# A convolution over edges: messages kept in PSUM, the radial layers moved two groups ahead, chunk sums turned in the messages' banks

## The chip, the core and the metric

The kernel runs on one core of one Trainium2 chip. The metric is the device time of one execution in microseconds (us). Before the change three runs took 5604.22, 5641.0 and 5611.24 us; the median is 5611.24.

The engines are called as in the profile: PE is TensorE (matmuls; PEld its weight loads), DVE is VectorE, ACT is ScalarE, POOL is GpSimd, SP is SyncE. In this kernel SP only issues DMAs and POOL issues the gathers (indirect DMAs).

## What is computed

Two graph layers over 6250 nodes of 128 features and 200000 edges, sorted by destination. The first is a pair of attention layers. The second, the one that is changed, is a convolution over the edges. Cut to what matters:

```python
h = maximum(layernorm(x), 0)
e0, e1 = f0[src], f1[src]            # the source node's features, 32 and 32 x 3, after a linear map
a0, a1 = attr4[:, 0], attr4[:, 1:4]  # four attributes of each edge
h = gelu(gelu(attr8 @ W_mlp1) @ W_mlp2)        # two layers on eight more attributes
w = einsum('pxu,ex->epu', W_tp, h)             # third layer: four weights of 32 each
m0 = w[:, 0] * e0 * a0
m1 = w[:, 3] * (e1 * a1).sum(-1)
m2 = w[:, 1] * e0 * a1                          # 3 x 32
m3 = w[:, 2] * e1 * a0                          # 3 x 32
agg = zeros.at[dst].add(concatenate([m0, m1, m2, m3]))    # 256 sums for each node
out = cos * s + sin * (agg @ Wf)                # s: a linear map of the node itself
x = x + out
```

Each edge so needs one gathered row of 128 numbers, three small matrix products, 256 products and one addition into its destination.

## The kernel before, in words

The attention layers fill the first 2430 us and are not touched, but for the pool from which their one-hot tiles come. The convolution reads `table3` (the mapped features of every node) from device memory.

The 200000 edges lie in 1563 tiles of 128, one edge in each partition. Eight tiles are a **group** (195 full groups, and one of three tiles). Thirty tiles are a **chunk**: the edges of a chunk go to nodes that lie within 128 of the chunk's first one, so one accumulator of 128 x 512 in PSUM (`whole`, one buffer) holds the sums of a chunk. There are 53 chunks.

For each group, in the program's order (`convolve`, from line 1236):

1. POOL issues eight gathers (`gather`, line 319), each of 128 rows of `table3` into `G` (six buffers).
2. PE and ACT run two layers: a matmul of 512 columns (line 1244), a gelu (1246), again a matmul (1248) and a gelu (1250). The matmuls write `small` tiles, two buffers of one bank. The third layer is sixteen or so matmul instructions of 128 columns (1256) into `pw`, shown as `big`: 128 x 1024 in two banks, two buffers.
3. ACT scales each tile of `G` by `a0` into `g0` (1267, eight operations).
4. DVE forms the products: `dot` = e1 * a1 (1269), its sum (1271), `w1` = w * e0 (1273), two products into `mid`, 128 x 1024 in SBUF (1274, 1275), and two in place into `big` (1278, 1279). `mid` and `big` together are the group's messages.
5. `halve` splits a number into a rounded part and a remainder, so that the scatter's matmuls may run in their faster format: ACT copies into the first half (335), DVE subtracts that from the number into the second (336). This is done for `mid`, then the one-hot tile of the next group is made (`one_hot`, 328, shown as `ohr`), then it is done for `big`.
6. PE scatters: for each tile one matmul of 512 columns (1286) with the one-hot tile as weights, added in `whole`. The two halves of messages lie beside each other and are added later.

At a chunk's end (`close`, `sums3`) ACT copies 256 columns of `whole` (1313) and DVE adds the other 256 (1314). The next chunk's first matmul into `whole` waits for that. In the seventh tile of the next chunk the sums are carried into its accumulator by a matmul with a shifted one-hot tile (`same`, 1344 and 1345). One group later `finish3` (1291) turns the sums by two transposes (1295, into a `small` tile), ACT copies them (1297), PE multiplies by `Wf` (1300) and DVE scales by sin and adds the node's own part `xb`, which SP loaded, in two operations (1303, 1304). SP stores the result.

SP issues, for each group, two loads of `attr8` (`a8t`, four buffers), for each five groups a load of `attr4` (`a4`, three buffers), for each chunk the load of `xb` and the store. DVE copies the three attributes `a1` of five groups from `a4` into PSUM (1362), in a bank `kept` that also holds the column numbers `slot` which `one_hot` compares with.

The order of instructions on each engine is set when the kernel is built: a scheduler takes the program's order as priority and puts an instruction earlier on its engine where it expects that engine free and the operands ready. Each engine runs its list strictly in that order, and waits are semaphores. A new tile in a pool waits until the last readers of the buffer that it takes over are done.

Of the kernel before, what the change touches and what calls it, by code (L numbers as in the profile page):

```python
# [42 lines left out]
P = 128  # L43
SB = 8
# [22 lines left out]
def gnn_kernel(ctx: ExitStack, tc: tile.TileContext, x, src, dst, attr4, attr8,  # L67
# [255 lines left out]
    def one_hot(dl, n, exact=True):  # L323
        if exact:
            oh = work.tile([P, SB, P], F32R, name="ohr", bufs=3)
        else:
            oh = gen.tile([P, GSB, P], F32, name="ohg")
        nc.vector.tensor_tensor(oh[:, :n, :], slot[:, None, :].to_broadcast([P, n, P]),
                                dl[:, :, None].to_broadcast([P, n, P]), op=OP.is_equal)
        return oh  # L330
# [26 lines left out]
    def attend(G, dl, n, oht, pq, H, acc_of, start, stop):  # L357
# [3 lines left out]
        oh = one_hot(dl, n)  # L361
# [24 lines left out]
    def attend_general(G, dl, n, erc, H, acc, start, stop):  # L386


        oh = one_hot(dl, n, False)
# [23 lines left out]
    def node_max(G, dl, n, H, most):  # L413

        oh = one_hot(dl, n, False)
# [633 lines left out]
    ps_big = ctx.enter_context(tc.tile_pool(name="ps_big", bufs=2, space=PSUM))  # L1049
    ps_sm = ctx.enter_context(tc.tile_pool(name="ps_sm2", bufs=2, space=PSUM))  # L1050
    ps_two = ExitStack()
    ps_bank = ps_two.enter_context(tc.tile_pool(name="ps_bank2", bufs=1, space=PSUM))
# [179 lines left out]
    kept = ctx.enter_context(tc.tile_pool(name="ps_kept", bufs=1, space=PSUM)).tile([P, 512], F32, name="kept")  # L1232
# [3 lines left out]
    def convolve(G, n, a0, a1, a8t, sink, oh, then=None):  # L1236


# [4 lines left out]
        ph = small()  # L1243
        nc.tensor.matmul(ph[:, :npr * P], wm1_sb[:rows], a8t[:rows, :npr * P], start=True, stop=True)  # L1244
        hid1 = cw.tile([2 * HID, NPR * P], F32, name="hid1")
        nc.scalar.activation(hid1[:, :npr * P], ph[:, :npr * P], AF.Gelu_apprx_tanh, scale=1.0 / math.sqrt(NRAD))  # L1246
        ph = small()
        nc.tensor.matmul(ph[:, :npr * P], wm2_sb, hid1[:, :npr * P], start=True, stop=True)  # L1248
        hid2 = cw.tile([2 * HID, NPR * P], F32, name="hid2")
        nc.scalar.activation(hid2[:, :npr * P], ph[:, :npr * P], AF.Gelu_apprx_tanh, scale=1.0 / math.sqrt(HID))  # L1250
        pw = big()

        for j in range(npr):
            for c in range(j, n, NPR):
                half = slice(c // NPR * HID, (c // NPR + 1) * HID)
                nc.tensor.matmul(pw[:, c, :], hid2[half, j * P:(j + 1) * P],  # L1256
                                 wtp_sb[half].rearrange("x p u -> x (p u)"), start=True, stop=True)
        w = pw[:, :n, :].rearrange("e c (p u) -> e c p u", p=4)
        m = cw.tile([P, SB, 4, MUL], F32, name="mid")
# [13 lines left out]
        nc.vector.tensor_tensor(w1[:, :n], w[:, :, 1, :], e0, op=OP.mult)  # L1273
        nc.vector.tensor_tensor(m[:, :n, 0, :], w[:, :, 3, :], dot1[:, :n], op=OP.mult)
        nc.vector.tensor_tensor(m[:, :n, 1:, :], w[:, :, 2, :][:, :, None, :].to_broadcast(s4),  # L1275
                                g0[:, :n, MUL:].rearrange("e c (i u) -> e c i u", i=3), op=OP.mult)

        nc.vector.tensor_tensor(w[:, :, 0, :], w[:, :, 0, :], g0[:, :n, :MUL], op=OP.mult)
        nc.vector.tensor_tensor(w[:, :, 1:, :], w1[:, :n, None, :].to_broadcast(s4),  # L1279
                                a1[:, :, :, None].to_broadcast(s4), op=OP.mult)  # L1280
        halve([ms[:, :n, j, 1] for j in range(2)], m[:, :n])
        got = then and then()
        halve([ms[:, :n, j, 0] for j in range(2)], w)
        for c in range(n):
            acc, start, stop = sink(c)
            nc.tensor.matmul(acc, oh[:, c, :], ms[:, c].rearrange("e s h i u -> e (s h i u)"), start=start, stop=stop)  # L1286
        return got

    sin = math.sin(math.pi / 8.0) / math.sqrt(2.0 * MUL) / math.sqrt(20.0)

    def finish3(a, xb, to):

        pt = small()
        for j in range(2):
            nc.tensor.transpose(pt[:, j * D:(j + 1) * D], a[:, j * D:(j + 1) * D], ident)
        at = cw.tile([P, 2, D], F32, name="at")
        nc.scalar.copy(at, pt[:, :2 * D].rearrange("p (j f) -> p j f", j=2))
        ps = small()
        for j in range(2):
            nc.tensor.matmul(ps[:, :D], at[:, j, :], wf_sb[:, j, :], start=j == 0, stop=j == 1)  # L1300
# [153 lines left out]
```

## Time and profile before

| | |
|---|---|
| median of the runs | 5611.24 us |
| the profiled execution, its own time | 4542.56 us |
| span of the profiled execution | 4540.8 us |
| busy over the span: PE, DVE, ACT, POOL | 70%, 77%, 63%, 61% |
| convolution: first gather to the end | 2433.2 to 4540.8 us |
| PE clock granted in the convolution | 0.72 of full |

A line of a group reads: line of the kernel, engine, operation, output <- inputs, sizes, count | busy us, mean ns of one | idle us of the engine just before them, and what ended the idle time. A line of waits reads: who waited <- for whom: us in total, times, longest us. A line of the timeline reads: start in us, duration in us, engine, line, operation, tiles, count and, in brackets, the idle time before it. DMA issues on POOL (`DMA_INDIRECT`) are shown with the time in which POOL makes them, not with the time in which the data moves.

### The profile page before, as it was taken

What the parts mean: (1) busy time and instruction counts of PE and PEld (TensorE: products, weight loads), DVE (VectorE), ACT (ScalarE), POOL (GpSimd) and SP (SyncE); (2) the same over time, 40 slices, a digit from 0 to 9 for tenths busy, and PEclk for the clock granted to TensorE, in tenths of its full rate; (3) what the DMA queues carried; (4) which work ended last, traced back from release to release, by engine and by line L of the source; (5) the groups of instructions that cost most, each with busy time, mean ns of one, the idle gap of its engine ahead of it and who ended that gap; (6) DMA issues with size and microseconds to landing.
All of it is one profiled execution on the core that took longest, in us unless ns stands there. A gap on an engine that the chain in (4) does not pass through costs nothing. (4 is left out here: it accounts for less than half of the span.)

```text
span 4540.8 us, 65437 instructions
## 1 busy us (share of the span) xinstructions
PE 3179.3 (70%) x21547; PEld 2348.1 (52%) x21548; DVE 3500.0 (77%) x5690; ACT 2880.8 (63%) x6866; POOL 2767.3 (61%) x2684
## 2 busy tenths in 40 slices
PE   4026576666766676599996777777777777778777
PEld 3015566656666566588883444444444444444444
DVE  5258678878887787688886878878778887877877
ACT  2025678788787788599995555555555555555554
POOL 0767776767767662100004777777777777777774
PEclk9998666666666676699997777767776767767776
DMA  4255555555555554644441222222222222222221
GB/s 110 67 141 148 149 150 160 159 147 159 165 167 154 156 156 128 217 157 152 158 159 53 60 59 59 59 58 62 57 58 58 59 58 57 59 58 58 58 57 33
DMA packets 348025, 480.87 MB, mean 106 GB/s; under 512 B 190601, under 2 KB 236207, under 8 KB 343694
## 3 DMA queue, kind: packets, MB, share of 16 engines
q1 hardware_dynamic: 199014, 238.86, 17.2%
q0 software_dynamic: 85776, 147.31, 13.6%
q10 hardware_dynamic: 62872, 90.28, 5.7%
q8 instruction: 176, 2.88, 0.3%
q14 instruction: 187, 1.53, 0.1%
HBM read 367.21 MB, written 108.97 MB: 105 GB/s over the span
## 5 line engine op out<-in xcount | busy, mean ns | idle before, releaser
L319 POOL DMA_INDIRECT G<-table,srcc x1563 | 1579.5, 1011 | 1003.1 <-DVE kept L1234 527.1
L319 POOL DMA_INDIRECT G<-table,srcw x1054 | 1116.6, 1059 | 514.1 <-issue 284.1
L1286 PE MATMUL whole<-halves,ohr 128*128 128x512 f32 x1563 | 671.8, 586 | 367.5 <-DVE halves L336 320.8
L889 ACT ACTIVATE ramp<-erb,sel 128x256 bf16<-128x256 f32 x1764 | 757.3, 499 | 15.8 <-DVE up L891 13.7
L1286 PEld LDWEIGHTS whole<-halves,ohr 128*128 128x128 f32 x1563 | 416.2, 280 | 604.3 <-DVE halves L336 392.5
L1267 ACT ACTIVATE g<-G,a 128x128 f32<-128x128 f32 x1563 | 516.3, 395 | 84.1 <-DMA G<-table,srcc 75.2
L1185 ACT ACTIVATE ramp<-erb,sel 128x256 bf16<-128x256 f32 (+1 forms) x1225 | 491.7, 498 | 22.8 <-DVE up L1189 16.7
L784 ACT CAST ca<-small 128x392 bf16<-128x392 f32 x784 | 343.2, 482 | 191.8 <-PE small L782 181.7
L909 PE MATMUL up<-rc,up 128*128 128x102 bf16 x3528 | 313.8, 265 | 169.7 <-DVE up L891 168.2
L909 PEld LDWEIGHTS <-up 128*128 128x128 bf16 x3528 | 269.1, 130 | 197.4 <-DVE up L891 191.2
L782 PE MATMUL small<-key,lo 128*128 128x98 bf16 x3136 | 312.8, 250 | 79.6 <-ACT ca L784 70.8
L1256 PEld LDWEIGHTS big<-wtp_sb,hid 64*128 64x128 f32 x3126 | 255.6, 238 | 198.2 <-ACT hid L1250 96.6
L381 PE MATMUL whole<-halves,ohr 128*128 128x136 f32 x1054 | 229.1, 368 | 179.2 <-DVE halves L336 126.3
L891 DVE TENSOR_TENSOR up<-ramp,ctc 128x1792 bf16<-128x1792 bf16 x252 | 273.7, 1087 | 84.5 <-ACT ramp L889 71.2
L1248 PE MATMUL small<-hid,wm_sb 128*128 128x512 f32 x392 | 280.2, 804 | 81.2 <-ACT hid L1246 81.0
L336 DVE TENSOR_TENSOR halves<-big,halves 128x1024 fp32r<-128x1024 f32 x196 | 237.8, 1213 | 123.3 <-ACT halves L335 123.1
L1256 PE MATMUL big<-wtp_sb,hid 64*128 64x128 f32 x3126 | 305.4, 342 | 27.0 <-ACT hid L1250 27.0
L771 DVE TENSOR_TENSOR lo<-slots,turned 128x2048 bf16<-128x2048 bf16 x196 | 239.3, 1221 | 110.0 <-PE small L782 106.5
L335 ACT CAST halves<-mid 128x1024 fp32r<-128x1024 f32 x196 | 204.1, 1041 | 166.9 <-DVE mid L1275 165.1
L1246 ACT ACTIVATE hid<-small 128x512 f32<-128x512 f32 x196 | 116.9, 596 | 298.8 <-PE small L1244 298.7
L782 PEld LDWEIGHTS <-lo 128*128 128x128 bf16 x3136 | 244.7, 123 | 110.9 <-issue 98.5
L381 PEld LDWEIGHTS whole<-halves,ohr 128*128 128x128 f32 x1054 | 200.3, 274 | 191.6 <-DVE halves L336 134.7
(293 smaller groups left out, 6202.2 us busy)
## 6 DMA issues: line engine op xcount, KB each, us to landing
counts<-ca ACTq DMA_DIRECT2D x196, 392.0 KB
ct<-counts SPq DMA_DIRECT2D x192, 392.0 KB
rc<-rhs SPq DMA_DIRECT2D x63, 717.5 KB
oht<-dlow SPq DMA_DIRECT2D x31, 1088.0 KB
ctc<-counts SPq DMA_DIRECT2D x504, 56.0 KB
G<-table,srcc POOLq DMA_INDIRECT x1563
G<-table,srcw POOLq DMA_INDIRECT x1054
a8t<-attr_rows SPq DMA_DIRECT2D x391, 16.0 KB
```

The lines of the kernel that those rows point to most:

```text
L319: nc.gpsimd.indirect_dma_start(out=G[:, c, :], out_offset=None, in_=table, in_offset=bass.IndirectOffsetOnAxis(ap=idx[:, c:c + 1], axis=0))
L381: nc.tensor.matmul(acc, oh[:, c, :], ms[:, c].rearrange("e s f -> e (s f)"), start=start and c == 0, stop=stop and c == n - 1)
L782: nc.tensor.matmul(ps[:, k * NKEY:(k + 1) * NKEY], lo[:, a, :, r], ky[:, a, :, r], start=True, stop=True)
L784: nc.scalar.copy(ca[:, :, i * W:(i + WBANK) * W].rearrange("p h (k d) -> p h k d", d=W), ps[:, :WBANK * NKEY].rearrange("p (k h d) -> p h ...
L889: nc.scalar.activation(ramp[:, i, :n * P], erb[:, h, :n * P], AF.Relu, bias=sel1[:, h0 + i, h:h + 1], scale=STEEP)
L891: nc.vector.tensor_tensor(up[:, :, :n * P].rearrange("p h (a d) -> p h a d", d=QN), ramp[:, :, :n * P].rearrange("p h (a d) -> p h a d", d ...
L909: nc.tensor.matmul(ups[k][:, h], up[:, i, k * P:(k + 1) * P], by_head[:, i, :, h, :], start=h0 + i + h == 0, stop=h0 + i + h == NB + H1 - 2)
L1185: nc.scalar.activation(ramp[:, h, :n * P], erb[:, :n * P], AF.Relu, bias=sel2[:, h0 + h, :], scale=STEEP)
L1248: nc.tensor.matmul(ph[:, :npr * P], wm2_sb, hid1[:, :npr * P], start=True, stop=True)
L1256: nc.tensor.matmul(pw[:, c, :], hid2[half, j * P:(j + 1) * P], wtp_sb[half].rearrange("x p u -> x (p u)"), start=True, stop=True)
L1267: nc.scalar.activation(g0[:, c], G[:, c, :], AF.Copy, scale=a0[:, c, :])
L1286: nc.tensor.matmul(acc, oh[:, c, :], ms[:, c].rearrange("e s h i u -> e (s h i u)"), start=start, stop=stop)
```

## The change

Five things are done together.

- `mid` lies in PSUM now (tile `mess`, two banks, one buffer). The first layers' matmuls no longer write `small` tiles, which are gone, but the halves of the group's own `pw` tile, before its third layer is written there.
- `convolve` is cut into `layers` (a generator that stops after each layer), `messages` and `scatter`. The layers of group g + 2 are issued around the scatter of group g: layer 1, four scatter matmuls, layer 2, four scatter matmuls, layer 3. Two groups' layers run ahead of the loop.
- In `messages` the next one-hot tile is made ahead of the products into `mid`; ACT's copy of `mid` is followed by DVE's two products in `big`, ACT's copy of `big`, and then both of DVE's subtractions.
- At a chunk's end ACT copies all 512 columns and DVE adds nothing: both halves are carried by a matmul each, and turned by matmuls with the identity that add them up, into a `mess` tile. sin is multiplied into `Wf` once (`wo_sb`); `xb` is added by a matmul with the identity; ACT copies the result out, with no DVE operation.
- `a4` is loaded two stretches of five groups ahead; DVE's copy of `a1` into PSUM comes right after the messages of a stretch's last group.

The core of the diff:

```diff
+    ps_big = ctx.enter_context(tc.tile_pool(name="ps_big3", bufs=2, space=PSUM))
+    ps_kept = ctx.enter_context(tc.tile_pool(name="ps_kept", bufs=1, space=PSUM))
...
+    nc.scalar.activation(wo_sb[:, :, :MUL], wf_sb[:, :, :MUL], AF.Copy, scale=sin)
...
-        ph = small()
-        nc.tensor.matmul(ph[:, :npr * P], wm1_sb[:rows], a8t[:rows, :npr * P], start=True, stop=True)
...
         pw = big()
+        hid = []
+        for j, (w, x, size) in enumerate(((wm1_sb[:rows], a8t[:rows], NRAD), (wm2_sb, None, HID))):
+            ph = pw[:, j * NPR:(j + 1) * NPR, :].rearrange("p c u -> p (c u)")[:, :npr * P]
+            nc.tensor.matmul(ph, w, (hid[-1] if j else x)[:, :npr * P], start=True, stop=True)
+            hid.append(cw.tile([2 * HID, NPR * P], F32, name=f"hid{j}"))
+            nc.scalar.activation(hid[-1][:, :npr * P], ph, AF.Gelu_apprx_tanh, scale=1.0 / math.sqrt(size))
+            yield
...
+        yield pw
+
+    def messages(G, n, a0, a1, pw, then):
...
-        m = cw.tile([P, SB, 4, MUL], F32, name="mid")
+        m = ps_kept.tile([P, SB, 4 * MUL], F32, tag="mess", name="mess").rearrange("e c (p u) -> e c p u", p=4)
...
         nc.vector.tensor_tensor(w1[:, :n], w[:, :, 1, :], e0, op=OP.mult)
+        got = then and then()
         nc.vector.tensor_tensor(m[:, :n, 0, :], w[:, :, 3, :], dot1[:, :n], op=OP.mult)
...
+        nc.scalar.copy(ms[:, :n, 0, 1], m[:, :n])
...
-        halve([ms[:, :n, j, 1] for j in range(2)], m[:, :n])
-        got = then and then()
-        halve([ms[:, :n, j, 0] for j in range(2)], w)
+        nc.scalar.copy(ms[:, :n, 0, 0], w)
+        nc.vector.tensor_tensor(ms[:, :n, 1, 1], m[:, :n], ms[:, :n, 0, 1], op=OP.subtract)
+        nc.vector.tensor_tensor(ms[:, :n, 1, 0], w, ms[:, :n, 0, 0], op=OP.subtract)
...
+        ps = ps_kept.tile([P, SB, P], F32, tag="mess", name="turned3")[:, :2, :]
         for j in range(2):
-            nc.tensor.transpose(pt[:, j * D:(j + 1) * D], a[:, j * D:(j + 1) * D], ident)
+            for i, a in enumerate(parts):
+                nc.tensor.matmul(ps[:, j, :], a[:, j * D:(j + 1) * D], ident, start=i == 0, stop=i == len(parts) - 1)
...
+            nc.tensor.matmul(ps[:, 0, :], at[:, j, :], wo_sb[:, j, :], start=j == 0, stop=False)
+        nc.tensor.matmul(ps[:, 0, :], ident, xb, start=False, stop=True)
...
+        nc.scalar.copy(o, ps[:, 0, :])
...
-            state["sums"] = sums3(state["acc"])
+            a = cw.tile([P, 2, 2 * D], F32, name="acc3")
+            nc.scalar.copy(a.rearrange("p s f -> p (s f)"), state["acc"])
+            state["sums"] = [a[:, j] for j in range(2)]
...
+        for g, (t, n) in enumerate(groups):
...
+            gather(G, table3, srcc[:, t:t + n], n)
+            ms, after = messages(G, n, a4[:, cs, 0:1], a1s[:, cs, :], pws.popleft(),
+                                 (lambda: hots(g + 1)) if g + 1 < len(groups) else None)
+            if i + SB == LT and t + SB < NT:
+                a1s = keep_a1(t + SB)
+            finish()
+            ahead = weights(g + 2) if g + 2 < len(groups) else iter(())
+            next(ahead, None)
+            scatter(ms, oh, range(0, min(n, NPR)), lambda c: sink(t + c))
+            next(ahead, None)
+            scatter(ms, oh, range(min(n, NPR), n), lambda c: sink(t + c))
+            pws.extend(ahead)
+            oh = after
```

## The prediction

> **What bounds the kernel now.** I read the page first (busy shares), then the gathers of the last stage by their tile, then the waits, the timeline and the groups by shape, each inside that stage. The change touches only the convolution, which runs from 2433 us to the end.
>
> The page has no engine full over the span, so it does not say what sets the pace. The view of tile G does: POOL issues all 1563 gathers of the convolution.
>
> ```profile
> L319 POOL DMA_INDIRECT G<-table,srcc x1563: 940/945/1896, 2433.2 to 4487.6; - x196
> ```
>
> Median 945 ns, longest 1896. (4487.6 - 2433.2) / 1562 is 1.315 us from one gather to the next, 10.5 us for a group of eight. From 2700 to 4500 us the waits say what POOL idles for, and what VectorE idles for:
>
> ```profile
> POOL G L319 <- issue: 372.0, 1221, 0.3
> ...
> DVE halves L336 <- ACT halves L335: 164.9, 75, 4.7
> ...
> DVE w L1273 <- PE big L1256: 119.6, 32, 6.9
> ```
>
> POOL's idle time is its own 0.30 us between instructions; nothing there is a wait for a free G. So the least period is 0.945 + 0.30 = 1.25 us (the median period over the trace is 1.249), and 1.315 - 1.249 = 66 ns a gather come from long ones. The timeline shows when those occur:
>
> ```profile
> 3505.80 1.22 DVE L336 TENSOR_TENSOR halves<-mid,halves 128x1024 fp32r<-128x1024 f32 x1
> 3506.11 1.73 POOL L319 DMA_INDIRECT G<-table,srcc  x1 [0.30 <-issue]
> ...
> 3515.23 1.23 DVE L336 TENSOR_TENSOR halves<-mid,halves 128x1024 fp32r<-128x1024 f32 x1 [0.47 <-ACT halves L335]
> ...
> 3515.64 1.64 POOL L319 DMA_INDIRECT G<-table,srcc  x1 [0.30 <-issue]
> ```
>
> A gather that starts during the subtraction of halves from mid (both in SBUF) ends 0.82 us after the subtraction (3506.11 + 1.73 = 3507.84 against 3507.02). Counted over the trace: 162 of 1563 gathers exceed 1.1 us, every one overlaps that one instruction, and all end 0.81 to 0.83 us after it. The long ones cost 101.9 us above 945 ns each. The same subtraction from big (in PSUM), as long, delays none.
>
> The second pace is that of the computing engines. From the start times: group 10's last gather starts at 2545.6 and its last scatter ends 26.3 us later; group 190's starts at 4441.2 and the scatter ends 48.7 us later. So gathers run at (4441.2 - 2545.6) / 180 = 10.53 us a group, and computing at 10.53 + 22.4 / 180 = 10.655. Both are nearly in balance; the six G buffers hide the difference to the end. Freeing POOL alone would gain almost nothing. VectorE's need, from the groups by shape (3000 to 4000 us, 94 groups):
>
> ```profile
> L336 DVE TENSOR_TENSOR halves<-mid,halves 128x1024 fp32r<-128x1024 f32 x94 | 114.7, 1220 | 27.4 <-ACT halves L335 27.3
> L328 DVE TENSOR_TENSOR ohr<-kept,dstc 128x1024 fp32r<-128x1024 f32 x94 | 114.5, 1218 | 0.0
> L336 DVE TENSOR_TENSOR halves<-big,halves 128x1024 fp32r<-128x1024 f32 x94 | 114.4, 1216 | 67.4 <-ACT halves L335 67.4
> ...
> L1273 DVE TENSOR_TENSOR w<-big,G 128x256 f32<-128x256 f32 x94 | 39.4, 419 | 68.5 <-PE big L1256 67.8
> ```
>
> and from the table by stretches:
>
> ```profile
> 3200.00:3700.00 500.00, 380.34 (x1396) 217.59 (x1396) 400.71 (x528) 261.47 (x590) 384.82 (x379) 0.71 0.22 58
> ```
>
> (PE, PEld, DVE, ACT, POOL busy, then PE's clock.) VectorE is busy 400.7 / 500 x 10.55 = 8.45 us of a group; the remaining 2.1 us are the waits, 67.4 + 27.4 + 68.5 = 163.3 us in 94.8 groups or 1.7 us, and small ones.
>
> [...] The trace: the VectorE subtractions are alike (1220 and 1216 ns), ScalarE's copy is 44 ns shorter from PSUM (1044 to 1000). [...] The trace has both levels only, half for 56% of the convolution, and every PE price has two values: a scatter matmul's median is 396 ns at full, 628 at half.
>
> **The change, part by part.**
>
> *mid in PSUM.* No two-SBUF operation of VectorE is left in the stage's steady part. Taken away: 162 blockings, 101.9 us. The writes of mid cost as the like forms to big do (960 against 947 ns, 432 against 422): +0.02 us a group; ScalarE's copy -0.04. Bounds: 0 if the block were by the destination, 102 if by the inputs; the PSUM form's freedom speaks for 102.
>
> *Both halves' subtractions behind the products.* ScalarE's copy of mid (1.0 us) now runs beside the two products of w (0.43 + 0.96), that of big beside the subtraction of mid (1.22). The wait for copies, (67.4 + 27.4) / 94.8 = 1.0 us a group, goes, unless ScalarE is late: scalings and gelus queued in front of a copy would bring it back, at the full 1.0 us.
>
> *Layers two groups ahead.* Same matmuls, now into pw itself, between the halves of a scatter, so gelus lie beside scatters. PE begins layer 1 when VectorE ends group g and needs, at half clock, 2.07 + 2.07 + 2.08 for layers and 3.78 for the scatter (timeline): 10.0 us; VectorE asks for the result one period and about 2.4 us later (dot and its reduction first), 12.4 at gather pace. At full clock (1.1 + 1.1 + 1.2 + 2.1) it takes 5.5. So the wait for big, 0.7 us, goes; slack 2.4 us at worst. Queued behind layer 1 on PE, if VectorE is late, are the scatters, and behind them the chunk's accumulator.
>
> *Chunk end, 53 times, each 3.75 groups.* VectorE loses the add (0.42) and both output steps (0.19 + 0.28): -0.24 us a group. ScalarE copies 512 columns in place of 256 (0.37 to about 0.59, as an equal copy elsewhere) and writes o (about 0.25): hidden, ScalarE is busy 5.5 of 10.5 us (uncovered, 53 x 0.5 = 26 us). PE: the two transposes become four matmuls (eight instructions), one carry more, one for x. At full clock, by the timeline's 0.71 us for four such instructions, about 1.4 - 0.38 + 0.59 + 0.35 = 2.0 us a chunk; at half about 2.4 - 0.48 + 1.22 + 0.6 = 3.7; or +0.5 and +1.0 us a group. PE now is busy 0.76 x 10.5 = 8.0 us, so 8.8: under 9.99. mid's banks are shared with the turned sums: PE 1.4, copy 0.37, PE 1.1, copy 0.25 and four handovers, some 4 us, must end before the next mid product. VectorE has dot 0.95, reduction 1.03, w 0.42 and one-hot 1.22 = 3.6 us ahead of it and the last subtraction: at most 1 to 2 us late per chunk, against 3.75 x 1.6 us of spare.
>
> *Loads and start.* The same a8t, a4, x and output DMAs on SP, a8t and a4 issued earlier; gathers on POOL neither moved nor queued behind them. Two new ScalarE scalings at the start lie ahead of the first landed G. Zero; a microsecond if not.
>
> *Sum.* VectorE: 8.45 - 0.24 + 0.02 = 8.2 us; gathers 8 x 1.249 = 9.99. Gathers set the pace if waits stay below 1.75 us a group. Last gather at 2433.2 + 1562 x 1.249 = 4384 (was 4487.6): -103. After it, 4540.8 - 4487.6 = 53 us today, of which some 25 are the backlog; then 0.95 for the gather itself, 2.4 to land, 8.2 for the last full group, 3.7 for the three tiles that remain (timeline), 11.9 from the last subtraction to the end: about 27. So 4384 + 27 is 4411; I write 4412. Gain 129 us. The profiled execution took 4542.6, 1.8 around its span, so 4414.
>
> The runs shown have a median of 5611, 1.235 times the profiled one, and nothing on the page says where those 1069 us lie. If all is stretched alike the gain is 159 us (5452); if the rest is a fixed addition, 129 (5482). I take 5465.
>
> **Rivals.** *Computing stays the pace (0.23).* The waits return in another place: mid's banks at a chunk end, ScalarE's order, pw's two buffers. At 10.3 us a group: 195 x 0.355 = 69 us, 1.5%; at 10.7, 9 us lost. 5526 to 5622. For it: before, computing was the slower; against: both named waits are addressed and 1.75 us is spare.
>
> *PE at half clock (0.08), slower.* At half clock PE needs 10.0 + chunk ends (2.9 + 3.7) / 3.75 = 11.8 us a group; at full 5.5 + (1.7 + 2.0) / 3.75 = 6.5. If half windows cover more than about (10.655 - 6.5) / 5.3 = 0.78 of PE's work, PE decides; all of it: +223 us, 4764, or 5720 to 5890 scaled. [...]
>
> *The runs are bound by computing more than the profile (0.12).* If the 1069 us stretch computing and not POOL, removed waits count whole: 195 x 2.1 x 1.235 = 506 us, half of it if half stay: 5105 to 5360.
>
> *Gather pace (0.57)*: 5440 to 5510.
>
> **Numbers.** Over 1% faster: 0.57 + 0.12 + 0.05 of the first rival = 0.74; within 1%, about what a measurement can tell here, 0.18; slower 0.08. The range 5360 to 5615 leaves out the half clock and the large gain.
>
> **What would show it.** No gather above 1.1 us, period 1.25 us; waits for copies and for big nearly gone; lag between gather and scatter flat; about 25 to 30 us after the last gather. Wrong: POOL waiting for G's release, long gathers still there, or VectorE waiting on mess or PE.

## The result, and the profile after

| | before | changed |
|---|---|---|
| median, runs taken together | 5619.73 us | 5585.02 us |
| ratio, with its 95% interval | 1 | 0.9931 (0.9903 to 0.9958) |
| the same in a second comparison | 5627.53 us | 5583.49 us, 0.9924 (0.9903 to 0.9945) |
| span of a profiled execution | 5608.7 us (profiled again) | 5586.3 us |
| first gather of the convolution to the end | 2597.2 us | 2571.8 us |

The change is worth 0.7%, some 40 us; the forecast was 5465 us, or 2.6%.

One thing has to be known to read these numbers: the profiled execution of the kernel before that the prediction was built on (span 4540.8 us) was not like the timed runs. The same kernel profiled again has a span of 5608.7 us, as its runs have, and all later comparisons here are with that one.

The view of tile G shows it at once. First the changed kernel, then the kernel before, profiled again (count, then shortest/median/longest ns, then first and last start):

```profile
L319 POOL DMA_INDIRECT G<-table,srcc x1563: 938/945/962, 3014.5 to 5518.6; - x196
```

```profile
L319 POOL DMA_INDIRECT G<-table,srcc x1563: 938/944/1978, 3011.5 to 5543.7; - x196
```

The longest gather is now 962 ns: no gather is held any more, as forecast. But a gather takes (5518.6 - 3014.5) / 1562 = 1.603 us from one to the next, not 1.25, and in the kernel before 1.621, not the 1.315 of the first profile. And the convolution begins at 3014 and 3011 us in place of 2433, although the stages ahead of it are the same code. So the execution shown first lacked something that costs some 24% both ahead of the convolution (3011.5 against 2433.2 us) and in it (2597.2 against 2107.6 us). On which chip it ran is not on record.

What POOL, ScalarE and VectorE wait for in the changed kernel between 3200 and 5400 us (total us, times, longest):

```profile
POOL G L319 <- issue: 592.7, 1269, 12.7
...
ACT hid L1252 <- remote: 203.7, 47, 8.6
DVE halves L1293 <- ACT halves L1287: 184.3, 54, 10.4
ACT at L1309 <- remote: 172.6, 34, 8.0
DVE mess L1282 <- ACT o L1315: 156.8, 21, 13.4
...
DVE w L1280 <- remote: 110.5, 39, 6.7
```

and in the kernel before, the same stretch of its second profile:

```profile
POOL G L319 <- issue: 719.3, 1289, 15.9
...
DVE halves L336 <- ACT halves L335: 261.5, 52, 11.9
...
DVE w L1273 <- remote: 137.4, 31, 8.0
DVE w L1273 <- PE big L1256: 128.6, 31, 6.6
```

The reader is to see the last column: waits of 6 to 16 us, several times the length of any instruction in the loop (the longest on record there, a scatter product, takes 1.42 us). In the first profile (2700 to 4500 us) no wait of these three engines was longer than 7.6. "Remote" is the page's word for a release that it can tie to no instruction of this core. POOL's idle time (913 us of 2200) is more than its own 0.30 us for each of 1364 gathers, 409 us: it waits for free G buffers. The last gather of a group leads its scatter by 87 us through the whole stage (quartiles 84 to 89), where it was 26 us early in the first profile. Gathers are not the pace.

The timeline of the changed kernel around one chunk end shows how such a wait looks:

```profile
3529.11 1.23 DVE L1293 TENSOR_TENSOR halves<-mess,halves 128x1024 fp32r<-128x1024 f32 x1 [1.03 <-ACT halves L1287]
...
3530.39 1.16 PE L1307 MATMUL turned<-ident,acc 128*128 128x128 f32 x8 [0.58 <-issue]
3530.74 1.28 ACT L1274 ACTIVATE g<-G,a 128x128 f32<-128x128 f32 x4
...
3532.22 1.09 PE L1250 MATMUL big<-a8t,wm_sb 16*128 16x512 f32 x2 [0.67 <-issue]
...
3536.97 0.37 ACT L1309 COPY at<-turned 128x256 f32<-128x256 f32 x1 [4.95 <-remote]
...
3538.41 0.64 PE L1312 MATMUL turned<-xb,ident 128*128 128x128 f32 x2
...
3546.92 0.27 ACT L1315 COPY o<-turned 128x128 f32<-128x128 f32 x1 [7.13 <-remote]
...
3547.22 0.43 DVE L1282 TENSOR_TENSOR mess<-big,dot 128x256 f32<-128x256 f32 x1 [11.58 <-ACT o L1315]
```

TensorE's turning products end on record at 3531.55 and ScalarE, free since 3532.02, starts its copy of them at 3536.97; the trace has a count of TensorE's semaphore (the signal that a product is done) at 3536.95. The output's products end at 3539.05, and ScalarE copies them at 3546.92, right after a count at 3546.89. The prediction allowed 4 us from mid's release, the end of the subtraction in the first line, to the copied output; here it is 3547.19 - 3530.34 = 16.9.

Counted where ScalarE already stood waiting when TensorE's product ended on record (gelus and the copy `at`): 287 cases in the first profile from 2700 to 4450 us, none over 0.1 us; from 3200 to 5300 us 278 in the second profile of the kernel before, 42 over 1.5 us, and 288 in the changed kernel, 74 over 1.5 us, mean 0.92 us.

The counts of the semaphores tell whose handovers these are. From 3200 to 5400 us of the changed kernel, every count of ScalarE and of VectorE that is on record (1113 and 1138) comes within 0.01 us of the recorded end of an instruction of theirs. Of TensorE's 731 counts, 240 come more than 1.5 us after the last product that counts, up to 6.76 us. So in this trace late counts are TensorE's alone. In the first profile all 637 of TensorE's counts from 2700 to 4450 us come within 0.03 us. The profile models the end of a product, so the traces do not tell whether TensorE is done late or its signal comes late. The changed kernel's trace also lacks many counts (ScalarE has 1113 for 2179 instructions that count, in the first profile 2057 for 2066); whether the recording itself has a part in this, no run tests.

### The profile page after: what moved, and what is told of

It is laid out like the page before. It is cut to its first block, busy times and chain, and to the rows that moved or that the text cites. A ratio compares the mean times of both kernels' runs of the same rounds, so it can differ in the third digit from the quotient of the medians.

```text
span 5586.3 us, 66809 instructions
## 1 busy us (share of the span) xinstructions
PE 3395.3 (61%) x22075; PEld 2519.0 (45%) x22076; DVE 3498.1 (63%) x5531; ACT 2900.8 (52%) x6921; POOL 2639.6 (47%) x2684
## 5 line engine op out<-in xcount | busy, mean ns | idle before, releaser
L319 POOL DMA_INDIRECT G<-table,srcc x1563 | 1475.4, 944 | 1556.8 <-issue 676.6
L319 POOL DMA_INDIRECT G<-table,srcw x1054 | 1091.9, 1036 | 987.3 <-DVE w L362 384.4
L1300 PE MATMUL whole<-halves,ohr 128*128 128x512 f32 x1563 | 798.7, 647 | 24.3 <-issue 23.3
L1252 ACT ACTIVATE hid<-big 128x512 f32<-128x512 f32 x392 | 233.9, 597 | 951.5 <-PE big L1250 419.5
L778 PE MATMUL small<-key,lo 128*128 128x98 bf16 x3136 | 339.0, 260 | 484.3 <-ACT ca L780 213.3
L1300 PEld LDWEIGHTS whole<-halves,ohr 128*128 128x128 f32 x1563 | 418.1, 283 | 438.2 <-issue 373.7
L1250 PE MATMUL big<-a8t,wm_sb 16*128 16x512 f32 x392 | 294.5, 840 | 394.8 <-issue 346.6
L767 DVE TENSOR_TENSOR lo<-slots,turned 128x2048 bf16<-128x2048 bf16 x196 | 239.5, 1222 | 418.5 <-remote 206.0
L1293 DVE TENSOR_TENSOR halves<-mess,halves 128x1024 fp32r<-128x1024 f32 x196 | 239.1, 1220 | 350.6 <-ACT halves L1287 201.2
L1250 PE MATMUL big<-hid,wm_sb 128*128 128x512 f32 x392 | 356.7, 1011 | 112.4 <-ACT hid L1252 99.0
L377 PE MATMUL whole<-halves,ohr 128*128 128x136 f32 x1054 | 248.1, 388 | 173.1 <-issue 80.0
L377 PEld LDWEIGHTS whole<-halves,ohr 128*128 128x128 f32 x1054 | 218.3, 294 | 185.2 <-issue 84.5
```

The lines of the kernel that those rows point to most:

```text
L319: nc.gpsimd.indirect_dma_start(out=G[:, c, :], out_offset=None, in_=table, in_offset=bass.IndirectOffsetOnAxis(ap=idx[:, c:c + 1], axis=0))
L377: nc.tensor.matmul(acc, oh[:, c, :], ms[:, c].rearrange("e s f -> e (s f)"), start=start and c == 0, stop=stop and c == n - 1)
L778: nc.tensor.matmul(ps[:, k * NKEY:(k + 1) * NKEY], lo[:, a, :, r], ky[:, a, :, r], start=True, stop=True)
L1250: nc.tensor.matmul(ph, w, (hid[-1] if j else x)[:, :npr * P], start=True, stop=True)
```

## Experiments

Each kernel is the changed one with one edit, but for the first. "Against the changed kernel" is its ratio to the kernel before, measured on the same chip, divided by 0.9927 (the mean of the two ratios above); two such quotients that differ by less than some 0.4% are not told apart. The changed kernel was measured in two of these comparisons only; the kernel before took 5562 to 5628 us (medians) in the several ones, so on the other chips it is assumed that the ratio carries over. 1% is 56 us.

**The kernel before, profiled again.**

> The kernel before, unchanged, profiled beside the others. Theory H (late handovers): the runs shown are not paced as the profile of before was; a signal from one engine to another arrives microseconds late at times, in every stage. Then this execution takes about 5610 us, its convolution starts near 3010 us as in the changed kernel's profile (not at 2433), takes about 2600 us, and the page shows idle time that ends with a signal of unknown origin. Theory G (the profile of before is right and only the changed kernel's execution was disturbed): about 4545 us, convolution from 2433 us.

5610.51 us, span 5608.7, the first gather at 3011.5. The regime is that of the runs.

**What each part of the change is worth.** Three parts undone one at a time, and one left out.

```
e2:  m = cw.tile([P, SB, 4, MUL], F32, name="mid")         # SBUF, in place of the mess tile
e3:  nc.sync.dma_start(out[ds(first_node(c), P), :], xb)   # in place of finish3
e4:  pw = list(weights(g))[-1]; messages(...); scatter(ms, oh, range(n), ...)   # no layers ahead
e7:  copy and subtraction of mid behind the products of w, then the one-hot, then copy and subtraction of w
```

> The changed kernel with mid back in SBUF (the first part of the change undone). Theory H: gathers wait for their buffers most of the time and do not set the pace, so blocked gathers cost nothing: long gathers come back (about 160 above 1.1 us), and the time stays within 0.5% of the changed kernel's 5585 us, or falls a little, because the turned sums no longer share a buffer with mid (the wait of the product into mess for the output copy, 172 us in the changed kernel's trace, goes away; up to 150 us faster). Theory G (gather pace): some 100 us slower.

> The changed kernel without the turning and the last product of a chunk's sums: the node's own part is stored alone (this part of the computation is left out); the carry into the next chunk stays. Theory H with the chunk end as the cost: VectorE no longer waits for the output copy (172 us) before it writes mess, and PE has 14 instructions less a chunk: 150 to 250 us faster, 5340 to 5430 us. If the chunk end is hidden: within 1% of 5585.

> The changed kernel with the three layers of a group issued just ahead of its own messages and the scatter in one piece (layers two groups ahead undone). Theory H: layers ahead hide late handovers between PE and ScalarE, so this is slower, 5650 to 5900 us. If layers ahead bring nothing because the scheduler already moves them: within 0.5% of 5585.

> The changed kernel, but with the order of the kernel before around the copies: the two products into big first, then copy and subtraction of mid, the one-hot, copy and subtraction of big. The prediction's step (1.0 us a group of waits for copies goes with the new order) gives 195 us more at most, 5640 to 5780, ratio 1.003 to 1.03. If handovers set the pace whatever the order, within 0.5% of the changed kernel: 5560 to 5610. The old order has one thing for it: mess is first needed 2 us later after the last subtraction (the one-hot no longer lies there but the products do not move), so the wait of VectorE for mess should not shrink; if the time falls under 5550, the one-hot between the two copies covers more than it costs.

| kernel | ratio to before (95%) | against the changed kernel |
|---|---|---|
| mid in SBUF | 1.009 (1.0056 to 1.0124) | +1.6%, 92 us |
| no chunk output | 0.9713 (0.9674 to 0.9752) | -2.2%, 121 us |
| layers in place | 1.0014 (0.9993 to 1.0036) | +0.9%, 49 us |
| old copy order | 1.0014 (0.9988 to 1.0039) | +0.9%, 49 us |

Each of the three parts helps. Added up they make 190 us, and the whole change makes 40; if parts add, something in it takes about 150 back. Leaving out the chunk's output altogether brings 121, or 2.3 us for each of 53 chunks.

How mid in SBUF loses is instructive. Its rows by shape (busy and mean ns, then idle time before and what ended it), 3200 to 5400 us, first of the changed kernel, then with mid in SBUF:

```profile
L1293 DVE TENSOR_TENSOR halves<-mess,halves 128x1024 fp32r<-128x1024 f32 x171 | 209.2, 1223 | 309.2 <-ACT halves L1287 184.3 <-issue 80.3 <-ACT hid L1252 41.1
...
L1282 DVE TENSOR_TENSOR mess<-big,dot 128x256 f32<-128x256 f32 x171 | 72.6, 424 | 177.3 <-ACT o L1315 156.8 <-issue 20.4
```

```profile
L1293 DVE TENSOR_TENSOR halves<-mid,halves 128x1024 fp32r<-128x1024 f32 x166 | 203.2, 1224 | 513.7 <-ACT halves L1287 441.6 <-issue 41.0 <-ACT hid L1252 30.0
...
L1282 DVE TENSOR_TENSOR mid<-big,dot 128x256 f32<-128x256 f32 x166 | 69.0, 415 | 1.1
```

With mid in SBUF nothing shares the buffer of the turned sums, and VectorE's wait for it goes (177 to 1 us). But VectorE only gets sooner to the next place, the subtraction, and waits 204 us more there, for ScalarE's copy. During those of these waits that last over 1 us, ScalarE itself stood idle ahead of a gelu (212 us) and ahead of `o` (95 us), which come before that copy in its list. So the wait moved, and its removal alone brought no time. The gathers that are held again (65 of 1563, 36 us above 945 ns) can hardly explain the 92 us, since a group's last gather leads its scatter by 87 us here too; what explains them stays open.

**The shared buffer, or the form of the chunk's end?**

```
e5:  turned = kept[:, 2 * P:]     # the turned sums beside slot and the attributes, not in mess
e6:  the same, with sums3, the two transposes, wf_sb and VectorE's two output steps of the kernel before
```

> The changed kernel, but the turned sums and the output of a chunk have columns of their own (256 of the bank of slot and attributes, whose attributes are kept once in place of twice) and no longer share mess with the middle messages. The four PE products more, the copies by ScalarE and everything else stay. Theory S (the shared buffer is what a chunk's end costs: the changed kernel's trace has VectorE idle 171.6 us at the first product into mess, waiting for ScalarE's copy of o): 5425 to 5500 us, ratio to the kernel before 0.965 to 0.980, that wait gone, and about what leaving the chunk's output out gave (5466.7). Theory F (the form is what it costs: four products more on PE and two more turns between PE and ScalarE ahead of the scatters): 5560 to 5600, ratio 0.990 to 0.997; VectorE's wait moves to the scatters and to ScalarE's copies of halves.

> The same separate columns, and the chunk's end in the form of the kernel before: ScalarE copies 256 columns, VectorE adds the other 256, two transposes, one carry, two products with the unscaled weights, and VectorE scales and adds x with its two output steps. Left of the change: mid in PSUM, both subtractions behind the products, layers two groups ahead. Theory S: within 25 us of the kernel with separate columns and the new form, either way (VectorE +0.24 us a group, PE -0.5 to -1.0). Theory F: 60 to 120 us under that kernel, 5460 to 5530, ratio 0.972 to 0.984. If the parts add up by the runs so far (mid in PSUM 89 us, layers ahead 48), a whole old chunk end gives 5625 - 137 = 5488 or less.

> The changed kernel itself, for the comparison on this chip: 5560 to 5610 us, ratio to the kernel before 0.990 to 0.997 by every theory.

The changed kernel again: 0.9924. Sums beside slot: 0.9999 (0.998 to 1.0019), 0.7% slower. Old chunk end: 0.9867 (0.9832 to 0.9902), 0.6% faster. Theory S of the shared buffer misses its forecast, but the first of the two did not give the sums a place of their own. Among its waits:

```profile
DVE same L1345 <- ACT o L1316: 123.0, 34, 6.8
```

`same` reads `slot`, other columns of that bank; it is one tile, so VectorE now waits for the output there. The second has no such wait and no copy `o` on ScalarE, and it beats both kernels, if by little: 32 us under the changed one measured beside it. That is in the direction of theory F (74 us between the two), not at its size against the changed kernel. Since it gives up both the shared buffer and the new form, it does not tell the two apart.

**Only the place in the queues.** The same instructions, put between the layers' steps.

```
turning products | layer 1, gelu | copy at | half the scatter | output products, copy o | layer 2, gelu | other half
e9:  in free columns of the layers' own tile pw         e10: in mess, as in the changed kernel
```

> The changed kernel, with a chunk's turning and output taken apart and put between the steps of the layers, in the columns of the layers' own tile that are free at that time: turning products, layer 1, its gelu, ScalarE's copy at, half the scatter, output products, ScalarE's copy o, layer 2, its gelu, other half, products with wtp. Nothing of a chunk is in mess any more; the instructions are the same in number and kind. Theory Q (what a chunk's end costs is its place in the queues: ScalarE waits 195 us for the turned sums and 133 us for the output in 2200 us of the changed kernel's trace, with the gelu, the next group's scalings and copies behind it, and TensorE's layer 1 waits behind that): 5440 to 5520, ratio 0.967 to 0.981; waits of ScalarE at these two copies fall under half. Theory S (the buffer shared with mess): the same time, since it is no longer shared. Theory F (the four products more and the two copies as work): 5560 to 5600.

> The same staging, but the turned sums and the output stay in mess, which is now held for some 4 to 6 us longer at each of 53 chunk ends. Theory Q: 5460 to 5560, under the changed kernel (5585) although VectorE's wait for mess grows. Theory S: 5600 to 5750, over the changed kernel, since the hold of mess is what a chunk's end costs. The difference to the kernel staged in the layers' tile is the price of the sharing alone.

In pw 0.9985 (0.9966 to 1.0005), 0.6% slower than the changed kernel; in mess 0.9891 (0.9854 to 0.9929), 0.4% faster, which is within what can be told. Neither version tests theory S as meant. The one in mess does not hold the buffer longer: from the first turning product to the end of the copy `o` it is 10.0 us on average in both kernels, and VectorE's wait for mess is 3.4 us a chunk end in place of 3.9:

```profile
L1283 DVE TENSOR_TENSOR mess<-big,dot 128x256 f32<-128x256 f32 x177 | 75.1, 424 | 159.1 <-ACT o L1319 134.0 <-issue 20.6 <-DVE ohr L324 4.5
```

The one in pw holds a buffer of the layers in its place. Theory Q is not borne out: it had the version in pw at 0.967 to 0.981, with the waits at the two copies under half. In pw the wait at `at` is gone, and the wait at mess, but not the one at `o`:

```profile
L1253 ACT ACTIVATE hid<-big 128x512 f32<-128x512 f32 x333 | 199.0, 598 | 997.2 <-remote 511.5 <-PE big L1251 334.0 <-issue 98.0
...
L1283 DVE TENSOR_TENSOR mess<-big,dot 128x256 f32<-128x256 f32 x167 | 70.4, 422 | 0.0
...
L1312 ACT COPY at<-big 128x256 f32<-128x256 f32 x45 | 16.5, 366 | 0.0
L1319 ACT COPY o<-big 128x128 f32<-128x128 f32 x44 | 11.7, 266 | 205.1 <-remote 158.8 <-PE big L1316 23.0 <-PE big L1315 10.6
```

The gelus of the changed kernel wait 815.4 us in the same stretch, `at` 195.0, `o` 133.0, the copy of the accumulator 60.3: ScalarE waits 1204 us for TensorE. Here it is 997.2 + 0 + 205.1 + 28.3 = 1231. With mid in SBUF it is 1228, with layers in place 1222, with the old order 1231, with sums beside slot 1140, staged in mess 1154. That the sum stays within 6% follows from the times being so near each other with the same work on ScalarE. What the rows add is the place: one wait taken away comes back at another.

**Whose work sets the pace?** Four kernels leave work out.

```
e11: messages(..., None)                 # no one-hot after the first group
e12: if start or stop or c % 2 == 0: nc.tensor.matmul(acc, ...)     # half the scatter
e13: nc.scalar.activation(g0[:, :n], G[:, :n, :], AF.Copy, scale=a0[:, 0, :])   # one for eight
e14: layer 2 and its gelu left out
```

> The changed kernel with the one-hots left out after the first group (every scatter takes the first group's, so the sums go to other rows): VectorE has 1.21 us a group less to do, 236 us over 195 groups. If VectorE's work sets the pace: 5350 us, ratio 0.951. If the handovers between TensorE, ScalarE and VectorE set it: VectorE reaches the products into mess earlier and waits there or at ScalarE's copies instead, a gain of 30 to 120 us, 5465 to 5555, ratio 0.972 to 0.988. If the gathers' 1.249 us apiece set it (the forecast): no change.

> The changed kernel with nearly half of the scatter products left out (of a chunk's 30 tiles 16 are kept, the others' messages are lost): TensorE has some 385 us less to do in the convolution (0.467 x 704.4 us in 2200 us, over 2572 us), and no turn between engines goes. If TensorE's work sets the pace (its records end early): 5200 to 5330 us, ratio 0.925 to 0.948. If turns between the engines set it: 5480 to 5580, ratio 0.975 to 0.993. If ScalarE's work: no change.

> The changed kernel with one scaling of a whole group by the first tile's attribute in place of eight by their own (the other seven attributes are left out): ScalarE is busy some 2.2 us a group less (8 x 0.40 us against about 1.0 us as the copies of that size take), 430 us over the convolution. If ScalarE's queue sets the pace: 5200 to 5400, ratio 0.925 to 0.960. If TensorE or the turns set it, ScalarE waits more at the gelus and at the turned sums: 5520 to 5590, ratio 0.983 to 0.995.

> The changed kernel with layer 2 and its gelu left out (the products with wtp take the first layer's result): TensorE has some 370 us less to do (314 us in 2200), about as much as with half the scatters, and ScalarE 120 us; and one turn of a group from TensorE to ScalarE and back goes. If TensorE's work sets the pace: 5200 to 5350, the same as with half the scatters within 60 us. If the turns do: 5050 to 5250 and at least 200 us under the run with half the scatters.

| left out | work taken out | ratio to before (95%) | against the changed kernel |
|---|---|---|---|
| one-hots | VectorE, 236 us | 0.9815 (0.9781 to 0.9849) | -1.1%, 63 us |
| half the scatter | TensorE, 385 us at the price before | 0.9927 (0.989 to 0.9963) | 0 |
| seven of eight scalings | ScalarE, 279 us (not the 430 expected: 421.9 us in 163 groups became 184.2 in 159) | 1.0033 (1.0012 to 1.0053) | +1.1% |
| layer 2 | TensorE 370, ScalarE 120 us, and one turn | 0.9782 (0.9754 to 0.9809) | -1.5%, 82 us |

No engine's work alone sets the pace. Work taken from VectorE counts for a quarter of its size, from TensorE and ScalarE for nothing. Of two kernels with about as much TensorE work taken out, the one that also loses a turn, in which TensorE hands to ScalarE and gets the result back, is 82 us faster, less than the 200 that pure turns should have given (ScalarE's gelu goes too, but work on ScalarE counted for nothing). With one scaling the gelus just wait longer (775.4 to 956.1 us of 2100), and why the whole is 1% slower stays open.

Part of TensorE's answer is its clock. The stretch 3200 to 5300 us of the changed kernel and of the one with half the scatter (PE, PEld, DVE, ACT, POOL busy, with instructions, then the granted clock):

```profile
3200.00:5300.00 2100.00, 1435.28 (x5336) 852.56 (x5335) 1387.94 (x1704) 921.38 (x2084) 1228.98 (x1303) 0.70 0.18 48
```

```profile
3200.00:5300.00 2100.00, 1337.35 (x4723) 732.17 (x4722) 1381.52 (x1702) 919.79 (x2078) 1226.04 (x1300) 0.62 0.18 48
```

The kept scatters take 436.6 us in place of 673.1, 236 less, yet TensorE is busy only 98 us less, because at a clock of 0.62 in place of 0.70 most of its other products got longer: layer 1 went from 244.9 to 288.5 us with as many instructions. Its rows, of the changed kernel and with half the scatter:

```profile
L1250 PE MATMUL big<-a8t,wm_sb 16*128 16x512 f32 x325 | 244.9, 841 | 303.6 <-issue 271.5 <-remote 30.7 <-PE big L1258 1.3
```

```profile
L1250 PE MATMUL big<-a8t,wm_sb 16*128 16x512 f32 x326 | 288.5, 980 | 254.6 <-issue 214.5 <-remote 31.8 <-PE big L1258 8.3
```

**Filler on TensorE.** The opposite: products that only keep TensorE running. The "ticks" of the expectations are the counts of TensorE's semaphore.

```
def fill(): for _ in range(4): nc.tensor.matmul(kept[:, 3 * P:], ident, ident, start=True, stop=True)
e15, e16: 4 or 8 of them behind both layers' products and the turned sums
e18:      4 products of zeros added to the open accumulator instead, behind both layers' products
e17:      e10, with one half of the sums copied by ScalarE and the other added by VectorE
```

> The changed kernel with four products of the identity with itself, into columns nobody reads, behind each layer's first two products and behind the turned sums: TensorE gets about 4 x 0.33 = 1.3 us more to do twice a group and once a chunk, 590 us in all, and does not stand idle right after the products that ScalarE waits for. Theory I (ticks come late because TensorE is idle, and the clock is lower for it): 5250 to 5500 us, ratio 0.933 to 0.978, and the sum of late ticks well under the 600 us of the changed kernel in 3200 to 5300 us. Theory W (TensorE's work counts): 5750 to 6150. Theory L (late whatever TensorE does, with time to spare on TensorE): 5570 to 5700 and the same sum of late ticks.

> The same with eight products: 1200 us more for TensorE at 0.33 us each[...]. Theory I: about the same as with four or better, 5200 to 5500, with a granted clock above 0.8. Theory W or a full TensorE: 6000 to 6700. Theory L: 5700 to 6000.

> The changed kernel with four products of zeros with the identity, added to the open accumulator, behind each layer's first two products (twice a group): 390 times 4 x 0.33 = 1.3 us, about 510 us more work for TensorE, and no wait for another engine. Theory I (ticks are late because TensorE is idle): 5300 to 5520 us, ratio 0.943 to 0.982. Theory W (TensorE's work sets the pace at this place): 5950 to 6150, ratio 1.06 to 1.09. Theory L (late whatever TensorE does; TensorE has time to spare): 5570 to 5720, ratio 0.992 to 1.018.

> The staged chunk end in mess (5516.9 in its run, ratio 0.9891), with the sums as in the kernel before: ScalarE copies one half, VectorE adds the other, so two turning products in place of four and one carry in place of two. If the gain of the old chunk end came from TensorE's products: ratio 0.975 to 0.985. If VectorE's addition, which waits for ScalarE's copy in the middle of a group, costs as much: 0.986 to 0.996.

The first two took 1.0967 (1.089 to 1.1044) and 1.173 (1.1648 to 1.1812). Their times tell nothing of idle time: the filler writes the bank of `slot` and `a1`, and VectorE's first product of a group waits for it. The line is of the kernel with four:

```profile
DVE dot L1281 <- PE kept L1242: 571.1, 88, 10.5
```

Yet ScalarE's late starts grow rare in them: over 1.5 us are 30 of 263 with four and 5 of 237 with eight from 3200 to 5300 us, against 74 of 288 in the changed kernel.

In the accumulator the filler costs 1.0111 (1.0078 to 1.0144), 1.9% or 104 us over the changed kernel for about 510 us of work:

```profile
3200.00:5300.00 2100.00, 1568.80 (x7610) 1063.31 (x7609) 1356.15 (x1669) 905.35 (x2039) 1205.12 (x1275) 0.78 0.17 47
```

Its clock is 0.78. The filler was busy 413.1 us and TensorE in all only 1568.8 - 1435.3 = 133.5 more, so the useful products took 280 us less in this stretch; with 2% fewer groups in it, some 250 are left. The late starts did not go here: 99 of 340 over 1.5 us. Nor did they where the filler stands directly behind the product on TensorE, as it does for 139 of 160 second layers: 22 of 154 gelus of that layer start late, against 28 of 137 in the changed kernel. So a TensorE that has work behind the product is not enough to make its count come in time, and theory I falls as it was put; L is nearest (1.0111 lies in its 0.992 to 1.018). But "late whatever TensorE does" does not hold either, by the two kernels ahead; what in them makes the counts come in time stays open. The staged version with the old sums took 1.004 (1.0017 to 1.0064), 1.1% over the changed kernel, against both expectations. If the ratios of the several chips can be compared, VectorE's addition costs more there than TensorE's fewer products bring; the staged version in mess was not run beside it.

## Why the prediction was wrong

**The basis.** "Nothing on the page says where those 1069 us lie" was the weak place, and the text went on as if they could be scaled. 578 of them lie ahead of the convolution (3011.5 - 2433.2) and 490 in it, and with them come TensorE's late counts in both: ahead of the convolution 198 of 1431 in the second profile come over 1.5 us late, in the first 2 of 1499. With them the order of what is scarce is another one.

**Sum: "gathers set the pace at 9.99 us a group".** This is the step that failed. A group takes 1.603 x 8 = 12.8 us; in the timed regime the gathers wait for buffers before and after the change, and lead the scatters by 83 and 87 us. 1563 gathers at 1.249 us make 1952 us, and the convolution of the runs takes 2597: that could not be their pace. One-hots left out bring 63 us, where gather pace had no change.

**mid in PSUM, 101.9 us.** This part held: 162 long gathers in the first profile (153 in the second), none after, and the longest takes 962 ns in place of 1978. With mid back in SBUF 65 are long again, the longest 2001 ns. Why the subtraction from mid in SBUF holds a gather, no run shows. Undone it costs 92 us, near the forecast, but gathers did not set the pace and only 36 us of holding came back, so the agreement of the sizes is luck.

**Both halves' subtractions behind the products, 1.0 us a group.** The wait did not go. It is 309.2 us in 171 groups, 1.8 us a group, at the first subtraction. The prediction named the condition, "unless ScalarE is late", and that is what holds. The new order still brings 49 us of the 195.

**Layers two groups ahead, 0.7 us a group.** The wait for big is still there in another name: 216.2 us before line 1280 in 170 groups, 1.3 us a group, half of it ended by counts that the page ties to no instruction (110.5). Worth 49 us of the 137.

**Chunk end.** "At most 1 to 2 us late per chunk, against 3.75 x 1.6 us of spare" failed by size: the products into mess wait 177.3 us in 45 chunk ends, 3.9 us each, up to 13.4, and there is no spare. That wait is new, as the first rival named it. But removing it does not bring its time back (sums beside slot, staged in pw, mid in SBUF); each of these three puts another wait in, so the price of the shared buffer by itself is not shown. In its old form and in spare columns the chunk's end is 32 us cheaper. The parts do not add up: 190 us gained by three parts, 32 lost by the chunk's end, 40 net. Some 120 us of loss have no run of their own; parts of the change that were not tried alone, such as the layers' products in pw's own columns and `finish` ahead of the scatter, or mere interplay, are left.

**TensorE's price.** Forecast 8.8 us a group; measured 1435.28 us in 163 groups, 8.8. In part that is luck: in the kernel before, profiled again, it is 1340.76 us in 162 groups, 8.3 and not 8.0, so the change adds 0.5 and not 0.8. And it is without weight: half the scatter does not change the time.

**Rivals.** The one that came true is "computing stays the pace" (0.23, 5526 to 5622), in two of the three places it names, mess at a chunk's end and ScalarE's order. That its range holds is partly luck, since it worked with 10.3 us a group and 12.8 were measured. That "the runs are bound by computing more than the profile" was right as a statement and wrong in its consequence: the waits were thought to be removable whole. TensorE at half clock was not needed.

What is left as the pace is no engine's work but the ring of TensorE, ScalarE and VectorE, each of which runs its list in order and waits for the next (in the changed kernel ScalarE waits 1204 us of 2200 for TensorE), with handovers out of TensorE that are late by up to 6.76 us. This is argued from the traces and from what did not count, not shown by a run: the only kernels in which the late handovers grew rare (eight filler products in the bank of `slot`, and in part four) had a new wait in their place. Why TensorE's counts are late in the second profile and in the changed kernel's and not in the first, no run here shows.

## What to carry to other kernels

When the profiled execution and the timed runs differ by 20%, profile again before anything is costed: a wait that is the bound in one may be hidden in the other. In a loop where three engines hand work to each other, taking one wait away can move it to the next place in the ring (with mid in SBUF the 177 us at mess went, and 204 more stood at the subtraction), so price a change by what it does to the number of turns and to the lists that stand behind a turn, and give a removed wait or removed work a fraction of its size (here mostly from nothing to a third). Columns of the same PSUM tile are not separate buffers in this program: work on some columns made the readers of others wait, in three of these kernels (123.0 us at `same` with the sums beside slot, 571.1 and 800.8 us at `dot` with four and eight filler products). And look at how complete and how prompt each engine's counts are before a wait is blamed on the engine that waits.

## What the runs showed of the hardware

TensorE's time was elastic here. The size of the effect was not expected. In 2100 us, with 236 us of scatter taken out the granted clock fell from 0.70 to 0.62 and 138 us came back in other products; with 413 us of filler put in it rose to 0.78 and the others took 280 us less, some 30 of them for want of groups. Some 60% of the added busy time were made up, and more than half of the removed came back. The busy time alone does not give the clock: in the same stretch the kernel before, profiled again, is busy 1340.76 us at a clock of 0.68, the one with half the scatter 1337.35 at 0.62. What sets it, no run here shows.

The rounded halves do make the scatter's products the faster ones: at half clock a scatter product, 512 columns of halves, is one instruction of 628 ns (median, first profile), a carry's of 256 columns, not rounded, two of 634.

The late handovers were the other surprise, and that they are TensorE's alone: in the changed kernel 240 of its 731 counts come over 1.5 us late in 2200 us, while the recorded counts of ScalarE and VectorE come within 0.01 us of an instruction's end. In the timeline ScalarE stood idle for 7.13 us with the product it needed done on record, while POOL's gathers beside it went on every 1.25 us up to 3543.61. In the first profile none of 287 such handovers took over 0.1 us. With eight filler products behind the layers in the bank of `slot` 5 of 237 took over 1.5 us, with filler in the accumulator 99 of 340.
